# A recommender's GRU phase in program order on all engines, with a reordered phase change and a wider AUGRU tail

## Chip, cores and metric

One core of one Trainium2 chip. The metric is the device time of one execution in microseconds (us), median over the timed runs. Spans, busy times and waits come from the profile of one execution each. The experiments fell on three chips, called A, B and C here; the kernel before takes 2296 to 2299 us on chip A and 2259 to 2261 us on B and C (medians). The chip of the first runs of the two kernels is not recorded; their timed runs agree with chip A's. So kernels of different chips are compared by their ratio to the kernel before in the same rounds, or by stages of their profiles.

Shorthand for engines: PE is TensorE, DVE VectorE, ACT ScalarE, POOL GpSimd, SP SyncE.

## The reference

1024 users, 100 time steps, vectors of 128. A GRU runs over the history; an attention network scores every GRU state against the item; a masked softmax over time gives weights; a second GRU (AUGRU) runs over the GRU's states with these weights; its state at each user's own length goes into a small prediction network.

```python
def gru_step(h, x_t):
    gi = x_t @ gru_Wih.T + gru_bih
    gh = h @ gru_Whh.T + gru_bhh
    ...
    r = sigmoid(i_r + h_r); z = sigmoid(i_z + h_z)
    n = tanh(i_n + r * h_n)
    return (1.0 - z) * n + z * h
keys = scan(gru_step)                                       # 100 steps
feat = concatenate([keys, q, keys - q, q * keys])           # q: the item
score = relu MLP 512 -> 80 -> 40 -> 1 of feat, masked
pooled = einsum('bt,btd->bd', softmax(score over t), keys)
att_seq = pooled.T[:T]
def augru_step(h, (x_t, a_t)):
    r = sigmoid([h, x_t] @ Wr.T + br); u = sigmoid([h, x_t] @ Wu.T + bu)
    h_hat = tanh([h * r, x_t] @ Wh.T + bh)
    u = a_t[:, None] * u
    return (1.0 - u) * h + u * h_hat
hist_sum = (history * mask).sum(1) / length
comb = [user, item, hist_sum, item * hist_sum, AUGRU state at length - 1]
out = sigmoid MLP 640 -> 200 -> 80 -> 1 of comb
```

## The kernel before: the parts concerned

Users lie in the free dimension, in two halves of 512 columns. In the GRU phase a step does the gates of both halves and, one step later, the attention of both (`attend`). The three layers of the attention network for three successive time steps share one PSUM tile, in groups of 32 columns of the weights.

```python
def gru(self, t):                       # one half, one step
    pr = gate(0, both)
    nc.scalar.activation(r, pr, AF.Sigmoid, ...)
    ...
    pz = gate(1, both)
    nc.scalar.activation(pz, pz, AF.Sigmoid, ...)
    u = (ph + bhh) * r                  # VectorE, scalar_tensor_tensor
    nc.vector.tensor_add(pi, pi, u)
    nc.scalar.activation(pi, pi, AF.Tanh, ...)
    nc.vector.tensor_sub(d, h, pi)
    nc.vector.tensor_mul(d, pz, d)
    nc.vector.tensor_add(hn, pi, d)     # the new state
...
def attend(t):                          # 32 matmul records
    ...
    for half in halves:
        nc.vector.tensor_add(f, p[half.i], q0[...])
        nc.scalar.activation(half.mv, f, AF.Relu)
        half.score(t)                   # nc.scalar.dma_start: mv row -> s_b
...
for s in range(T):
    ...
    for half in halves:
        half.load(s + 2); half.load_mask(s + 2)   # x and m, by SyncE
        half.gru(s)
        half.product(s - 1); half.transpose(s - 1)  # kq; keys
        if half.i: attend(s - 1)
        half.stage()                    # softmax, one piece
        ...
        half.history(s)                 # GpSimd: hist += x * m
        half.pool(2, nc.gpsimd)         # GpSimd: pooled += e * key
...
with ExitStack() as pools:
    gru_phase(pools)                    # a scheduler orders the engines
```

The masks come late, so x and m of the first six steps are loaded a second time for `history` (called "again" below). AUGRU sorts users by length and narrows its columns from step to step (`WIDTHS`).

## Time and profile before

| | before |
|---|---|
| timed, median (4 runs) | 2299.15 us (2291.01 to 2299.93) |
| first profile: span, mean granted clock | 2260.6 us, 0.960 |
| last hn of the GRU phase | 1540.8 us |
| last hn to the end of AUGRU step 2 | 87.9 us |
| AUGRU step 2 to the end of the span | 631.9 us |

The lines of this profile are in the prediction. The profile is 1.7% shorter than the timed runs.

### The profile page before, as it was taken

The numbers are of one execution on the slowest core, as the hardware profiler recorded it, in microseconds if no ns is written. First come the engines' busy times: TensorE is split into PE (matmuls) and PEld (weight loads), VectorE is DVE, ScalarE is ACT, GpSimd is POOL, SyncE is SP. The second block draws the span as 40 slices with busy tenths as digits, with TensorE's granted clock in tenths as the row PEclk, the third lists the DMA queues.
The fourth block names the chain that finished last, engine by engine and source line by source line (L and its number), as shares of the span: only waits on it lengthen the run. The fifth ranks groups of instructions, "written<-read, shape, count | busy, mean of one in ns | idle before, by whom it ended". The sixth has DMA issues, their size and how long they took to land. (4 is left out here: it accounts for less than half of the span.)

```text
span 2260.6 us, 26532 instructions
## 1 busy us (share of the span) xinstructions
PE 2124.9 (94%) x8260; PEld 1013.4 (45%) x8260; DVE 1728.9 (76%) x3166; ACT 868.3 (38%) x1545; POOL 1285.2 (57%) x1289
## 2 busy tenths in 40 slices
PE   8898688999999999999999999995899999999998
PEld 3333233333333333333333333332444555679888
DVE  6776667788888888787878787898467877879752
ACT  3233223343433334333333333442343444445542
POOL 0147597676767676767676767694544444443410
PEclk9999899999999999999999999998899999999975
DMA  5344433332332323232323233312533333333310
GB/s 116 64 90 129 127 94 108 99 96 86 95 92 84 105 70 115 74 115 71 109 78 98 77 94 90 92 45 72 149 93 108 97 89 98 101 96 80 82 37 5
DMA packets 253427, 204.64 MB, mean 91 GB/s; under 512 B 74727, under 2 KB 215755, under 8 KB 253275
## 3 DMA queue, kind: packets, MB, share of 16 engines
q1 hardware_dynamic: 239482, 169.03, 27.7%
q0 software_dynamic: 12192, 32.17, 4.9%
q10 hardware_dynamic: 1600, 1.64, 0.2%
q8 instruction: 67, 1.10, 0.2%
q14 instruction: 86, 0.70, 0.1%
HBM read 146.73 MB, written 54.40 MB: 89 GB/s over the span
## 5 line engine op out<-in xcount | busy, mean ns | idle before, releaser
L463 PE MATMUL ps<-x,wih 128*128 128x512 f32 x1200 | 604.1, 613 | 62.2 <-ACT r L475 29.0
L463 PE MATMUL ps<-hn,whh 128*128 128x512 f32 x1188 | 583.2, 600 | 1.3 <-DVE hn L498 1.3
L463 PEld LDWEIGHTS ps<-x,wih 128*128 128x128 f32 x1200 | 220.0, 192 | 396.1 <-issue 214.1
L463 PEld LDWEIGHTS ps<-hn,whh 128*128 128x128 f32 x1188 | 228.4, 193 | 294.0 <-issue 267.6
L704 ACT ACTIVATE mv<-f 128x512 f32<-128x512 f32 (+1 forms) x204 | 128.2, 629 | 495.3 <-DVE f L703 371.7
L450 POOL TENSOR_TENSOR xm<-x,m 128x512 f32<-128x512 f32 x200 | 249.1, 1262 | 102.1 <-PE ps L463 72.6
L494 ACT ACTIVATE ps<-ps,bih 128x512 f32<-128x512 f32 x200 | 132.2, 661 | 400.7 <-DVE ps L493 324.4
L620 POOL TENSOR_TENSOR pooled<-pooled,kw 128x512 f32<-128x512 f32 x190 | 262.9, 1383 | 6.9
L451 POOL TENSOR_TENSOR hist<-hist,xm 128x512 f32<-128x512 f32 x200 | 263.7, 1333 | 2.9
L496 DVE TENSOR_TENSOR d<-hn,ps 128x512 f32<-128x512 f32 x198 | 135.7, 685 | 165.4 <-ACT ps L494 161.5
L605 POOL TENSOR_TENSOR pooled<-pooled,e 128x512 f32<-128x512 f32 x25 | 29.8, 1193 | 366.4 <-ACT e L579 366.4
L679 PE MATMUL pm<-hn,wk 128*32 128x512 f32 x1200 | 230.5, 600 | 6.0 <-DVE f L703 3.4
L152 POOL DMA_INDIRECT rows<-keys_d,idx_k x204 | 196.3, 962 | 69.3 <-issue 35.5
L679 PE MATMUL pm<-kq,wkq 128*32 128x512 f32 x1200 | 227.4, 594 | 0.0
L679 PE MATMUL pm<-mv,w 128*32 128x512 f32 (+1 forms) x808 | 213.5, 606 | 13.4 <-ACT mv L704 10.6
L530 DVE TENSOR_TENSOR kq<-hn,item 128x512 f32<-128x512 f32 x200 | 205.9, 1035 | 4.5 <-PE pm L679 4.3
L619 POOL TENSOR_TENSOR kw<-kt,e 128x512 f32<-128x512 f32 x190 | 207.4, 1110 | 0.5 <-DVE old L586 0.3
L483 DVE SCALAR_TENSOR_TENSOR u<-ps,bhh,r 128x512 f32<-128x512 f32 x198 | 145.8, 737 | 62.9 <-ACT r L475 53.7
L151 POOL COPY rows<-u 128x1 f32<-128x1 f32 x200 | 30.7, 181 | 258.4 <-DVE u L845 257.9
L497 DVE TENSOR_TENSOR d<-ps,d 128x512 f32<-128x512 f32 x200 | 137.9, 689 | 16.0 <-ACT ps L480 0.9
L493 DVE TENSOR_TENSOR ps<-ps,u 128x512 f32<-128x512 f32 x200 | 138.9, 694 | 13.5 <-PE ps L463 0.5
L835 PE MATMUL ph<-r,wh 128*128 128x512 f32 (+55 forms) x396 | 137.1, 430 | 9.5 <-DVE r L841 7.9
(154 smaller groups left out, 3167.0 us busy)
## 6 DMA issues: line engine op xcount, KB each, us to landing
x<-in_hist_x SPq DMA_DIRECT2D x212, 256.0 KB
keys_d<-kt SPq DMA_DIRECT2D x46, 1024.0 KB
m<-mask_d SPq DMA_DIRECT2D x200, 128.0 KB
keys_d<-kt SPq DMA_DIRECT2D x64, 64.0 KB
rows<-keys_d,idx_k POOLq DMA_INDIRECT x204, 2.8
s_b<-mv ACTq DMA_DIRECT2D x200, 8.0 KB
mask_i<-in_mask SPq DMA_DIRECT2D x8, 200.0 KB
at<-att_d SPq DMA_DIRECT2D x4, 256.0 KB
```

The source lines that it names most:

```text
L152: nc.gpsimd.indirect_dma_start(out=r[:, k, :], out_offset=None, in_=keys_d[q], in_offset=bass.IndirectOffsetOnAxis(ap=idx_k[:, k, i : i + ...
L450: nc.gpsimd.tensor_mul(d, x, m)
L451: nc.gpsimd.tensor_add(acc, acc, d)
L463: nc.tensor.matmul(p, lhsT=w[:, g, :], rhs=v, start=(j == 0), stop=(j == len(parts) - 1),)
L483: nc.vector.scalar_tensor_tensor(out=u, in0=ph, scalar=bhh[:, 2:3], in1=r, op0=ALU.add, op1=ALU.mult,)
L493: nc.vector.tensor_add(pi, pi, u)
L497: nc.vector.tensor_mul(d, pz, d)
L530: nc.vector.tensor_mul(kq, h, item[:, self.cols])
L619: eng.tensor_mul(d, k, w)
L620: eng.tensor_add(acc, acc, d)
L679: nc.tensor.matmul(p[i][s, :], lhsT=w[:, s], rhs=v, start=start, stop=stop)
L835: nc.tensor.matmul(p, lhsT=m[:, 0, :], rhs=v, start=False, stop=True)
```

## The change

Its intent: every engine executes the GRU phase in the order of the program text instead of a scheduler's, so attention matmuls are always issued in fours that share the array; preparation comes in small pieces, one per step; the poolings, features and weights at the phase change get a new order; AUGRU never has fewer than 96 columns, spreads its gathers evenly, and gives predictions two PSUM buffers of their own.

```diff
-EIGHTH, FALL = 8, 41
+EIGHTH, FALL, LEAST = 8, 41, 96
-WIDTHS = [[min(HB, 2 * -(-r // (2 * EIGHTH))) for r in room] ...
+    [max(LEAST, min(HB, 2 * -(-r // (2 * EIGHTH)))) for r in room] ...
 ... (preparation in yielded pieces, some of it moved to ScalarE)
-                nc.scalar.activation(pz, pz, AF.Sigmoid, bias=brz[:, 1:2])
 ... (in gru: z now follows tanh, kq stands inside the half)
                 nc.scalar.activation(pi, pi, AF.Tanh, bias=bih[:, 2:3])
+                nc.scalar.activation(pz, pz, AF.Sigmoid, bias=brz[:, 1:2])
+                between()
 ... (in the loop)
-        late = 6
+        late, again = 6, 24
-                half.gru(s)
-                if s:
-                    half.product(s - 1)
+            for half in halves:
+                half.gru(s, lambda: half.product(s - 1) if s else None)
+                if half.i == 0:
+                    for each in halves:
+                        each.stage()
+            for half in halves:
+                half.exponents()
 ...
+                for half in halves:
                     half.transpose(s - 1)
-                if s and half.i:
-                    attend(s - 1)
+                if not staged:
+                    next(rest, None)
+                attend(s - 1)
 ... (after the loop)
-            half.pool(T, nc.vector)
+        for half in reversed(halves):
             half.weights()
         for half in halves:
             half.features()
 ... (AUGRU)
-        ps = ... name="ps3", bufs=8, space=PSUM
+        ps = ... name="ps3", bufs=6, space=PSUM
+        pa = ... name="pa3", bufs=2, space=PSUM    # predictions, weights
-                for _ in range(RATE):
+                for _ in range(due.pop(0) if due else 0):
                     next(ahead, None)
-    with ExitStack() as pools:
+    with ExitStack() as pools, tc.manual_schedule():
         gru_phase(pools)
```

## The prediction

> **What bounds the kernel now.** I read the page's busy slices first, then busy time by stretch, then orders of time (timelines) of single steps, last the waits by engine. The stretches (columns: length, then busy us of PE, PEld, DVE, ACT, POOL, then granted clock, DMA share, GB/s):
>
> ```profile
> 1200.00:1500.00 300.00, 293.06 (x1138) 112.13 (x1140) 250.30 (x388) 119.33 (x184) 210.50 (x171) 0.99 0.32 92
> ...
> 2178.00:2190.00 12.00, 10.72 (x57) 9.86 (x55) 4.96 (x29) 3.91 (x15) 2.23 (x4) 0.64 0.09 24
> 2190.00:2247.00 57.00, 55.98 (x252) 54.09 (x253) 19.46 (x122) 17.48 (x66) 0.00 (x0) 0.50 0.03 6
> ```
>
> In the GRU phase TensorE is busy 98% and VectorE 83%; in the last 57 us of AUGRU the granted clock is 0.50. But 98% is not 98% of the work possible. A timeline of one step shows what the matmuls cost:
>
> ```profile
> 1006.52 1.88 PE L463 MATMUL ps<-x,wih 128*128 128x512 f32 x4
> ...
> 1008.23 1.02 PE L463 MATMUL ps<-hn,whh 128*128 128x512 f32 x2
> ...
> 1014.33 0.62 PE L679 MATMUL pm<-hn,wk 128*32 128x512 f32 x2
> ...
> 1014.35 0.62 PE L679 MATMUL pm<-mv,w 128*32 128x512 f32 x2
> ...
> 1014.79 0.60 PE L679 MATMUL pm<-hn,wk 128*32 128x512 f32 x2
> ```
>
> Four gate records take 1008.23 - 1006.52 = 1.71 us, 0.43 us each; well packed, four attention records of 32 columns start together every 0.43 to 0.46 us. A GRU step has 24 gate records (12 matmuls, two records each) and 32 attention records (the groups of costliest instructions: 3208 in 100 steps), so 24 + 32/4 = 32 slots of 0.43 = 13.7 us. The writes of hn give what a step takes: step 30 ends at 522.7, step 99 at 1540.8, 14.75 us each. So 1.0 us per step is lost to attention matmuls that come one by one. The first 31 steps took 522.7, some 65 us more than 31 times 14.75: preparation and DMA waits. From the last hn to the first full AUGRU step (PE at 1602.5) pass 61.7 us; AUGRU takes the remaining 658.
>
> **What the Trainium skill says.** "TensorE: Matmul & The Clock Gate", "Architectural detail": only PE may pull weight loads ahead; ScalarE and VectorE are strict FIFO. Here the order of two short queues decides everything. The same page, Part 1: little activity drops the clock to half; the trace agrees, 0.50 from 2190. "ScalarE: Activation LUTs", "What ACT_TABLE_LOAD costs": about 1283 ns plus a drain; the trace has 1.28. "SBUF — State Buffer", "Who interferes with whom": VectorE with two SBUF inputs blocks against GpSimd reads; the trace agrees: kq (two SBUF inputs) has median 0.82 but mean 1.035 and longest 1.74, while d, f and hn, each with an input in PSUM, stay at 0.65 to 0.69.
>
> **The change, part by part.**
>
> *GRU in program order.* The built order of the changed kernel is, per step, on VectorE: u, add, kq, d, d, hn for half 0, then a softmax stage if one is due, the same six for half 1, two transposes, two adds f. On ScalarE: r, tanh, sigmoid z for half 0, for half 1, exponentials if due, relu 0, its s_b DMA, relu 1, its DMA, then the next r. That closes a loop: the next u stands behind both f and needs r, and r stands behind both relus and DMAs, which need f. Its length comes from these lines:
>
> ```profile
> 251.93 0.71 DVE L483 SCALAR_TENSOR_TENSOR u<-ps,bhh,r 128x512 f32<-128x512 f32 x1
> 252.74 0.70 DVE L493 TENSOR_TENSOR ps<-ps,u 128x512 f32<-128x512 f32 x1
> 254.17 0.69 DVE L496 TENSOR_TENSOR d<-hn,ps 128x512 f32<-128x512 f32 x1 [0.73 <-ACT ps L494]
> 254.96 0.69 DVE L497 TENSOR_TENSOR d<-ps,d 128x512 f32<-128x512 f32 x1
> 255.69 0.69 DVE L498 TENSOR_TENSOR hn<-ps,d 128x512 f32<-128x512 f32 x1
> ```
> ```profile
> 1007.33 1.28 DVE L703 TENSOR_TENSOR f<-pm,q 128x512 f32<-128x512 f32 x2
> ...
> 1008.04 0.63 ACT L704 ACTIVATE mv<-f 128x512 f32<-128x512 f32 x1 [3.51 <-DVE f L703]
> 1008.69 1.28 ACT L475 ACT_TABLE_LOAD   x1
> ```
> ```profile
> 1026.39 0.50 ACTq L540 DMA_DIRECT2D s_b<-mv  x1
> 1026.94 0.63 ACT L704 ACTIVATE mv<-f 128x512 f32<-128x512 f32 x1 [5.83 <-DMA m<-mask_d]
> ```
>
> One half: u to add 0.81, add to d 1.43 (tanh in between, which kq fills), then 0.79, 0.73 and 0.61 until something independent may start: 4.37. Two halves 8.74, two transposes 2 x 0.635, two f 1.28: 11.29 of VectorE. After the start of the pair, f 0 ends at 0.68, relu 0 runs 0.71 to 1.34, its DMA holds the queue 0.50 (second fence of ScalarE: the next instruction starts 0.55 after the DMA), relu 1 1.92 to 2.55, DMA to 3.08, r 3.13 to 3.82, u at 3.86: 2.58 after the pair's end. A step without softmax is 11.29 + 2.58 = 13.87 us, already level with TensorE's 13.7. Softmax adds to it, because the stage stands in VectorE's row: scores 0.72 + 0.27 + 0.27 + 0.17 + 0.16 + 0.28 = 1.87, sums 0.33 + 0.25 + 1.01 + 0.93 = 2.52 (mean durations of the groups from 500 to 1500), both for two halves in 8 steps: +1.10. The table reload ahead of r: 1.28 x 2/8 = +0.32. kq under contention: I take +0.2. Sum: 15.5 us per step, **longer than the 14.75 of now**. TensorE's loss of packing goes away, but it will wait instead.
>
> Sum of the phase: hn of step 0 at 17 (16.7 now), 99 x 15.5 = 1534, less 14 for some ten early steps without softmax, plus 19 for preparation left on VectorE (8 rank counts 10.1, on 1.9, order 1.8, used 1.2, alive 1.0, small ones 3), plus 8 for the early steps in which s_b's DMA waits behind key writes: last hn at 1564, **+23** against 1540.8. The first 31 steps gain some 40 of it, the other 69 lose 52 and more. The pieces do remove the two 12 to 13 us stalls of now (idx_k waiting 12.4 for place_i, a d waiting 12.9).
>
> *Phase change.* Two queues for 8 pooled_d writes (6.6 us of issue on one now) and fewer separate softmax ends; but the features, now spread into the GRU's end, come after, with four GpSimd products of 1.28 ahead of the gathers. **-5.**
>
> *AUGRU on 96 columns.* Order of time of the h writes, half by half:
>
> ```profile
> 2160.97 0.26 DVE L851 TENSOR_TENSOR h<-h,ph 128x108 f32<-128x108 f32 x1
> ...
> 2164.27 0.26 DVE L851 TENSOR_TENSOR h<-h,ph 128x102 f32<-128x102 f32 x1
> ...
> 2185.96 0.22 DVE L851 TENSOR_TENSOR h<-h,ph 128x72 f32<-128x72 f32 x1
> ...
> 2191.92 0.22 DVE L851 TENSOR_TENSOR h<-h,ph 128x66 f32<-128x66 f32 x1
> ```
>
> At 102 columns a step takes 3.30 us, at 66 to 72 it takes 5.96, because the clock has halved. Steps 83 to 99 take 82.4 us now; 17 at 3.45, the rate of 98 columns, are 58.7: **-24**, if 96 keep the clock.
>
> *Gathers and PSUM.* Steps 8, 15, 22 and 30, at ends of blocks of keys, take 1.5 to 2.4 us over the trend; the even spread ends the gathers a step earlier: **-7**. Steps 27, 52 and 77, with the final predictions, are 5.5 to 7.3 us over it; with buffers of their own the predictions interleave with gates in the built order: **-9**. Six buffers instead of eight suffice for gates (three per half step).
>
> Sum: +23 - 5 - 24 - 7 - 9 = -22, so 2260.6 becomes 2239, -1.0%. The timed runs are 1.7% above the profiled one; with the same ratio 2299.66 x 0.990 = 2277. I say **2280**.
>
> **Rivals.**
> 1. TensorE sets the pace. Program order packs attention perfectly, and a step is 13.9: 99 x 13.9 + 17 + 19 = 1412, so -129 with -45 after: 2087, timed about 2125. For it: 98% busy and the purpose of the change. Against: TensorE is not in the loop worked out above; only durations that shrink could free it. In part (15.0 per step) it gives 2228 timed.
> 2. DMA waits move into ScalarE. Its s_b DMAs wait for earlier DMAs of the same semaphore; now they stop ScalarE, in order, for 76 us between 500 and 1500 (mv waiting, laid to m loads). If they stay, +0.7 per step: 2347. Against: GpSimd, whose lag delays the m loads now, has 10.5 us of work in a longer step, and loads are issued at the start of a step.
> 3. 96 columns do not hold the clock: the 24 are lost, 2304.
>
> **Range and chances.** The loop holds for given durations, so I do not see the GRU phase get much shorter; at 15.2 without contention all is 2245, at 16 some 2328. Unknown waits widen this: **2215 to 2330**. Faster by over 2% (below 2254) 0.25, within 2% 0.66, slower 0.09.
>
> **What would show it.** Right: hn writes 15 to 16 us apart in the middle, TensorE down to 88 to 90% there, idle mostly ahead of hn and kq matmuls; VectorE idle ahead of u by about 2.5 us each step, laid to r; first 31 steps faster, the rest slower; clock 1.00 at 2190 and after, steps of 3.4 to 3.5 at the end. Wrong: steps of 14 us or less with TensorE still at 98%, or ScalarE waiting for DMA by over 1 us per step.

## More of the kernel before

The stages are read off the timeline: a GRU step ends with its second write of hn, an AUGRU step with its second write of h.

The profiled execution took 2262.48 us and is none of the four timed ones; that is the time of chips B and C, and its stages fit theirs as well (see e5 and e15). So it may come from another chip than the timed runs; the record does not say.

## The result, and the profile after

The changed kernel takes 2373.7 us (2370.04 to 2380.84, 4 runs) against 2299.15. The ratio is 1.0336, with a 95% interval of 1.0303 to 1.037: slower by 3.4%. Ratios are the mean time of one kernel's fast runs over that of the other's of the same rounds, so not quite the ratio of the medians. The predicted 2280 and its range up to 2330 were too low. On chip C the changed kernel later took 2350.35 us, 1.0408 of the kernel before.

The profiled span is 2368.3 us. By stages, with a second profile of the kernel before from chip A beside the first:

| us | before, 1st profile | before, 2nd profile (chip A) | after |
|---|---|---|---|
| steps 1 to 24, mean | 17.37 | 17.23 | 15.81 |
| steps 25 to 48, mean | 14.61 | 14.61 | **17.36** |
| steps 49 to 95, mean | 14.83 | 14.81 | **15.74** |
| last hn | 1540.8 | 1537.2 | **1619.0** |
| last hn to AUGRU step 2 | 87.9 | 96.8 | **137.2** |
| AUGRU steps 3 to 83 | 539.4 | 563.4 | 543.0 |
| AUGRU steps 84 to 99 | 78.8 | 78.4 | 56.2 |
| span | 2260.6 | 2289.4 | 2368.3 |

Against the second profile, whose time is that of the timed runs, the change loses 82 us in the GRU phase and 40 at the phase change and gains 43 in AUGRU, some 79 in all. The medians of the timed runs differ by 75.

**The GRU phase.** The stretch of which the prediction shows the row of before, 1200 to 1500 us (columns as there):

```profile
1200.00:1500.00 300.00, 284.48 (x1096) 107.16 (x1094) 227.81 (x359) 110.57 (x168) 192.99 (x157) 0.98 0.29 85
```

TensorE is busy 284.5 of 300 us instead of 293.1, but with 1096 records instead of 1138: its busy time per record is no shorter (0.260 against 0.258 us). So the matmuls are not packed better here, and TensorE waits more.

The row of u in the groups of costliest instructions, before and after (behind the first bar busy time and mean duration, behind the second the idle time of VectorE ahead of it, with the releaser of most of it):

```profile
L483 DVE SCALAR_TENSOR_TENSOR u<-ps,bhh,r 128x512 f32<-128x512 f32 x198 | 145.8, 737 | 62.9 <-ACT r L475 53.7
```
```profile
L499 DVE SCALAR_TENSOR_TENSOR u<-ps,bhh,r 128x512 f32<-128x512 f32 x198 | 147.9, 747 | 328.9 <-ACT r L492 312.9
```

VectorE stood 62.9 us ahead of u in the whole phase, now 328.9, 3.3 us per step, and nearly all of it waits for r. An ordinary step shows the loop. Timeline of VectorE, then of ScalarE, around 1084 us (start, duration; in brackets the idle time before and what ended it):

```profile
1083.76 1.25 DVE L731 TENSOR_TENSOR f<-pm,q 128x512 f32<-128x512 f32 x2
1087.63 0.75 DVE L499 SCALAR_TENSOR_TENSOR u<-ps,bhh,r 128x512 f32<-128x512 f32 x1 [2.62 <-ACT r L492]
```
```profile
1084.44 0.63 ACT L732 ACTIVATE mv<-f 128x512 f32<-128x512 f32 x1 [3.48 <-DVE f L731]
1085.10 0.50 ACTq L558 DMA_DIRECT2D s_b<-mv  x1
...
1086.36 0.50 ACTq L558 DMA_DIRECT2D s_b<-mv  x1
1086.91 0.69 ACT L492 ACTIVATE r<-ps,brz 128x512 f32<-128x512 f32 x1 [0.58 <-PE ps L480]
```

The two f end at 1085.01; between them and r stand relu 0, its DMA, relu 1 and its DMA; u starts at 1087.63, 2.62 us after the f.

Steps 24 to 48 are another matter. Step 43, counted from 0, took 23.2 us (699.7 to 722.9). Its lines on SyncE's queue, ScalarE and VectorE:

```profile
684.20 0.42 SPq L455 DMA_DIRECT2D m<-mask_d  x1
705.88 0.33 SPq L450 DMA_DIRECT2D x<-in_hist_x  x1
```
```profile
701.56 0.63 ACT L732 ACTIVATE mv<-f 128x512 f32<-128x512 f32 x1 [4.23 <-DVE f L731]
708.95 0.50 ACTq L558 DMA_DIRECT2D s_b<-mv  x1
709.55 0.63 ACT L732 ACTIVATE mv<-f 128x512 f32<-128x512 f32 x1 [7.36 <-DMA m<-mask_d]
```
```profile
712.05 0.75 DVE L499 SCALAR_TENSOR_TENSOR u<-ps,bhh,r 128x512 f32<-128x512 f32 x1 [9.93 <-ACT r L492]
```

SyncE issues nothing for 21 us; relu 0 is done at 702.2, but its DMA goes out only at 708.95, after loads that SyncE issued at 705.88 and later; r and u follow. In these steps SyncE's queue waited 130.0 us for GpSimd's history products, which free the buffers of x and m (the waits of that queue, 395 to 812 us; 2.3 us from 812 to 1230). It waited longer for transposed keys, 160.8 us, but that is no less in the ordinary stretch (262.6). The sum alone says little: the kernel before has 239.7 us of waits for history products in the same window, but none over 8.7 us, where the longest here is 18.9.

What ties the two queues stands in the trace's own records of waits. A DMA raises a counter, its completion semaphore, when it lands. The DMAs of SyncE and ScalarE share eight of them, and 168 of the 200 s_b DMAs have a wait for their own semaphore right before them. The one of 708.95 waits for semaphore 104, on which the x load of 705.88 lands at 708.87; the one of 710.78 waits for semaphore 110, on which the x load of 706.78 lands at 710.71. So an s_b DMA is held until the load before it on its semaphore has landed.

**The phase change.** SyncE's queue and GpSimd, before and after:

```profile
1577.31 6.58 SPq L635 DMA_DIRECT2D pooled_d<-att  x8
```
```profile
1586.21 0.99 POOL L128 DMA_INDIRECT att_r<-pooled_d,idx  x1 [28.03 <-DMA pooled_d<-att]
```
```profile
1669.67 2.53 SPq L661 DMA_DIRECT2D pooled_d<-s_b  x4
1672.31 0.89 SPq L667 DMA_DIRECT2D rlen<-rlen_d  x1
...
1686.64 0.45 SPq L667 DMA_DIRECT2D rlen<-rlen_d  x1
...
1699.74 0.37 SPq L690 DMA_DIRECT2D part_d<-part  x1
```
```profile
1700.11 0.99 POOL L132 DMA_INDIRECT att_r<-pooled_d,idx  x1 [6.63 <-PE pk L868]
```

From the first pooled_d write to the first gather of weights pass 30.4 us instead of 8.9. The features of the two halves lie between, one after the other: the second rlen load stands in SyncE's order behind the part_d write of the first half. The pooled_d writes themselves begin 50.7 us after the last hn instead of 36.5. GpSimd has 19 pooling instructions left there instead of 13, and it waits for the softmax twice, 11.30 and 11.35 us; which of the two makes the 14 us is not shown. On chip C the same two pieces make up the whole difference: e13 (the changed kernel) against e14 (phase change of before) has 50.6 against 36.6, 29.2 against 8.9, and 118.8 against 84.7 in all.

**AUGRU.** The last steps keep their clock (columns as above):

```profile
2296.00:2355.00 59.00, 48.57 (x399) 45.62 (x397) 42.61 (x196) 29.07 (x102) 10.39 (x18) 1.00 0.26 41
```

### The profile page after: what moved, and what is told of

Read it like the earlier page. It is cut to its first block, busy times and chain, and to the rows that moved or that the text cites. A ratio compares the mean times of both kernels' runs of the same rounds, so it can differ in the third digit from the quotient of the medians.

```text
span 2368.3 us, 26550 instructions
## 1 busy us (share of the span) xinstructions
PE 2128.7 (90%) x8260; PEld 988.5 (42%) x8260; DVE 1727.8 (73%) x3155; ACT 873.3 (37%) x1547; POOL 1289.7 (54%) x1297
## 5 line engine op out<-in xcount | busy, mean ns | idle before, releaser
L480 PE MATMUL ps<-x,wih 128*128 128x512 f32 x1200 | 615.3, 623 | 28.6 <-ACT r L492 24.3
L499 DVE SCALAR_TENSOR_TENSOR u<-ps,bhh,r 128x512 f32<-128x512 f32 x198 | 147.9, 747 | 328.9 <-ACT r L492 312.9
L480 PEld LDWEIGHTS ps<-hn,whh 128*128 128x128 f32 x1188 | 233.2, 196 | 298.9 <-issue 295.1
L705 PE MATMUL pm<-kq,wkq 128*32 128x512 f32 x1200 | 221.8, 635 | 91.7 <-DVE kq L548 91.6
L732 ACT ACTIVATE mv<-f 128x512 f32<-128x512 f32 x200 | 125.9, 630 | 440.5 <-DVE f L731 349.1
L705 PE MATMUL pm<-mv,w 128*32 128x512 f32 (+1 forms) x808 | 219.2, 606 | 17.1 <-DVE e L587 14.8
L548 DVE TENSOR_TENSOR kq<-hn,item 128x512 f32<-128x512 f32 x200 | 194.8, 975 | 0.0
L492 ACT ACTIVATE r<-ps,brz 128x512 f32<-128x512 f32 x200 | 137.6, 688 | 56.7 <-PE ps L480 38.1
L884 PE MATMUL ph<-r,wh 128*128 128x96 f32 (+47 forms) x396 | 131.4, 414 | 19.6 <-DVE r L890 19.2
```

The source lines that it names most:

```text
L480: nc.tensor.matmul(p, lhsT=w[:, g, :], rhs=v, start=(j == 0), stop=(j == len(parts) - 1),)
L492: nc.scalar.activation(r, pr, AF.Sigmoid, bias=brz[:, 0:1])
L499: nc.vector.scalar_tensor_tensor(out=u, in0=ph, scalar=bhh[:, 2:3], in1=r, op0=ALU.add, op1=ALU.mult,)
L548: nc.vector.tensor_mul(kq, h, item[:, self.cols])
L705: nc.tensor.matmul(p[i][s, :], lhsT=w[:, s], rhs=v, start=start, stop=stop)
```

## The experiments

Unless said otherwise: correct, ratio to the kernel before of the same rounds.

### e1 to e4, chip A: is it the order, and is it the loop?

**e1_scheduled.**

```diff
-    with ExitStack() as pools, tc.manual_schedule():
+    with ExitStack() as pools:
         gru_phase(pools)
```

> The changed kernel with the scheduler let loose again on the GRU phase (only the program-order mode is taken away; pieces, order of code, phase change and AUGRU stay). Loop theory (the fixed order closes f, relu, DMA, relu, DMA, r, u into a loop): the GRU phase falls back to about 14.8 us per step, last hn at 1500 to 1550 instead of 1619, and the phase change gets back some 30 of its 49 us because the scheduler pulls features into the GRU's end; about 2250 to 2300 us. Rival (the rewritten code itself costs, e.g. z after tanh, kq inside the half, 'again' loads at 24): last hn stays above 1600 and the time near 2370.

Measured: 2210.88 us, ratio 0.961 (0.9573 to 0.9647). Last hn at 1487.7, means 14.75 (25 to 48) and 14.34 (49 to 95), phase change 104.4. The program-order mode alone costs the changed kernel 163 us, more than expected: the rewritten code, freely scheduled, is better than the kernel before. The rival (the rewritten code costs) is out.

**e2_before_gru_after_augru.** GRU phase and phase change of the kernel before, AUGRU of the changed one.

> GRU phase and phase change of the kernel before, AUGRU of the changed one (96 columns, even spread, PSUM buffers of its own for predictions). If the AUGRU part is worth what the changed kernel's trace shows from step 2 on (about 20 us), 2275 to 2282 us; if it is worth what the prediction gave it (40), about 2260. If its gain depends on the rest of the change (a GRU that ends late lets something finish), no change, 2299.

Measured: 2255.74 us, ratio 0.9803 (0.9767 to 0.984), so 43 us: about the 40 of the prediction, though its own profile (span 2262.1) is no shorter than the first profile of before. That contradiction led to e5.

**e3_before_program_order.** The kernel before with the program-order mode added, nothing else.

> The kernel before with program order alone for its GRU phase: nothing rewritten. Loop theory: program order is the cost and the rewriting a repair of part of it, so this is slower than the changed kernel: in each half product and transposes stand in VectorE's row ahead of the next half's u, z stands ahead of tanh in ScalarE's, and the preparation is in big lumps: 16 to 17.5 us per step, last hn 1650 to 1800, 2400 to 2550 us. If the rewriting costs and program order does not: faster than the changed kernel, about 2300.

Measured: 2800.54 us, ratio 1.2173, 20.18 us per step. The direction is right, the size far outside: the mode costs the unchanged code 502 us and the rewritten one 163, so the rewriting takes away most of the cost of program order. Which part of it does so was not taken apart.

**e4_f_and_relu_one_step_later.** Both f, both relus and their DMAs go into half 0 of the next step.

```diff
+                def between():
+                    if s:
+                        half.product(s - 1)
+                    if pend and half.i == 0:
+                        pend[0]()               # both f, behind kq
+                half.gru(s, between)
                 if half.i == 0:
                     for each in halves:
                         each.stage()
+                    if pend:
+                        pend[1]()               # relus and s_b DMAs, behind z
...
-                attend(s - 1)
+                pend = attend(s - 1, True)
```

> The changed kernel with both f, both relus and their s_b DMAs moved from the end of a step into half 0 of the next step (f behind kq, relus behind z), still program order. This opens the loop: the next r no longer stands behind relus that wait for f. Loop theory: outside the 'again' steps 24 to 48 a step falls from 15.8 to 14.2 to 14.6 us (VectorE's own 12.7, a bubble of 0.5 ahead of u of half 1, TensorE 13.7), last hn about 1480 to 1530, whole 2230 to 2290 us; VectorE's idle ahead of u falls from 3.3 us per step to under 1.5. DMA-wait theory (s_b DMAs waiting for loads stop ScalarE everywhere): the step stays near 15.8 since the same DMAs stand in the same queue ahead of r of half 1. In both, the spikes of 20 to 25 us in steps 24 to 48 stay.

Measured: 2226.47 us, ratio 0.9686 (0.965 to 0.9722), 147 us less than the changed kernel and a little better than expected. Last hn at 1463.6; means 14.42, 15.66 and 14.11 in the three stretches. The row of u:

```profile
L499 DVE SCALAR_TENSOR_TENSOR u<-ps,bhh,r 128x512 f32<-128x512 f32 x198 | 148.3, 749 | 190.6 <-PE ps L480 126.2
```

The wait is shorter, 1.9 us per step (under 1.5 was expected), and most of it is now for TensorE's matmuls, not for r: TensorE is the bound, busy 300.0 of 300 us from 1100 to 1400. The same DMAs stand in the same queue, so the DMA-wait theory does not explain the ordinary steps; but four of the five spikes of over 20 us in steps 24 to 48 are still there, with 19 to 25 us (27, 31, 35 and 43; step 47 has 14.5). A slip in this version, found later: the score of step 98 goes into a buffer whose block (92 to 95) has not been read yet. The comparison of results did not notice it; e9 repairs it.

### e5 to e8, chip A: the other terms

**e5_before_again.** The kernel before, unchanged.

> The kernel before, unchanged, profiled once more. Its first profile had a span of 2260.6 us at a mean clock of 0.960, but its timed runs took 2291 to 2309 at 0.950 to 0.956, while the changed kernel's profile and timed runs agree within 0.5%. If the difference lies in the narrow last steps of AUGRU (clock halved from an earlier step on), this profile is near 2298 us and the extra 38 us stand between step 60 and step 99, GRU unchanged (last hn at 1541). If it lies in the GRU phase, the last hn comes later than 1550.

Measured: 2299.68 us (2 runs), span of the profile 2289.4. The GRU phase is as before. The extra time is in AUGRU, but earlier than expected: steps 3 to 83 take 24.0 us more (563.4 against 539.4), steps 84 to 99 none (78.4). The phase change takes 9 more. Two stretches of it:

```profile
2140.00:2148.00 8.00, 5.58 (x40) 4.92 (x39) 5.06 (x20) 2.27 (x7) 6.58 (x13) 1.00 0.45 118
2148.00:2156.00 8.00, 5.80 (x27) 5.25 (x26) 3.69 (x14) 2.66 (x8) 1.86 (x2) 0.60 0.28 67
```

TensorE is busy only 5.58 of 8 us, and in the next 8 us its clock is 0.60: an idle stretch, and then, from 2149.6 for 6.8 us, half clock. The Trainium skill, "TensorE: Matmul & The Clock Gate", "HAM oscillation — how this bites in real kernels", has it that a wait that outlasts the activity window (some 3.4 us) makes the next work start cold. The trace agrees in part only: no single wait is that long here. The three before 2149.6 are 1.35, 0.80 and 0.82 us, and the one before the next half clock, at 2187.1, is 2.49. The clock is not all of the 24 us either: over steps 3 to 83 TensorE is idle 29.1 us instead of 13.4, and its busy time, with 23.9 us at half clock instead of 3.4, grows from 526.0 to 534.3. What makes it idle there is not shown.

The first profile has no such places between steps 53 and 83. All three profiles of kernels with common PSUM buffers on chip A have them (e3, e5, e6: 568.6, 563.4 and 565.8 for steps 3 to 83); the first profile, with 539.4, is nearer to those of chips B and C (e12, e15: 544.0 and 545.2, with the even spread). Its phase change, 87.9, is theirs too (86.8 and 87.6; 96.8 to 99.3 in e2, e5 and e6 on A).

**e6_before_with_96.** The kernel before with `max(LEAST, ...)` in `WIDTHS` alone.

> The kernel before with at least 96 columns alone (no even spread, no PSUM buffers of their own for predictions). If 96 columns are all of the gain of the AUGRU part (steps 2 to 83 of the changed kernel, 543.0 us, were no shorter than before, 539.4) and its other parts cost some 12 us at the start of AUGRU, this is at 2240 to 2252 us, faster than before's GRU with the whole new AUGRU part (2255.7). If the spread and the buffers are worth the 16 us that the prediction gave them, 2265 to 2275.

Measured: 2270.54 us, ratio 0.9878 (0.9859 to 0.9897): 26 us. Steps 84 to 99 fall from 78.4 to 58.2; steps 3 to 83 stay at 565.8, with the clock drops. The time lies in the second range, 2265 to 2275: 96 columns bring some 20 to 26 us, and spread and buffers together another 15 on this chip. They are not only the waits that the prediction meant: from e6 to e2 TensorE's idle time in steps 3 to 83 falls from 29.2 to 19.1 us, and its busy time, with fewer clock drops, from 536.6 to 524.2.

**e7_history_reload_own_buffer.** The second loads of x and m get a buffer pair of their own, one every four steps.

```diff
+        ag = pools.enter_context(tc.tile_pool(name="ag", bufs=1))
-                    x = xp.tile([P, HB], F32, name="x")
+                    x = (ag if again else xp).tile([P, HB], F32, name="x")
 ... (the same for m)
-            n, odd = divmod(s - again, 2)
+            n, odd = divmod(s - again, 4)
-            if 0 <= n < late and odd:
+            if 0 <= n < late and odd == 2:
                 halves[i].history(n)
```

> The changed kernel with the second loads of x and m of the first six steps in a buffer of their own and one every four steps (24 to 71) instead of every two (24 to 47); nothing else. DMA-wait theory for this stretch (the loads take buffers of the common rotation, so x loads of the coming step wait for GpSimd's history products of the step before; SyncE stands, and the s_b DMAs on ScalarE with it): the mean step of 24 to 48 falls from 17.36 to 15.8 to 16.0 us, spikes over 19 us go, last hn 1619 to some 1580 to 1585, whole 2330 to 2342 us. Rival (GpSimd's own load, not the buffers): the stretch keeps its mean of 17 or passes it to 48 to 72; no gain over 10 us.

Measured: 2345.59 us, ratio 1.0211 (1.0186 to 1.0236): 28 us less than the changed kernel. Steps 25 to 48 fall from 17.36 to 16.04 and steps 49 to 95 stay (15.73); last hn at 1587.6. No step of the stretch is over 19 us any more, and the slow stretch is not passed on to later steps. So the buffers and rate of the second loads cause it. The run changes both together and does not say which matters more.

**e8_features_ahead.** rlen and user loads right behind the loop; feature products on VectorE and matmuls ahead of the last poolings.

```diff
+        for half in halves:
+            half.ready()          # rlen and user loads
         for half in halves:
             half.product(T - 1)
...
         attend(T + 1)
+        for half in halves:
+            half.features()
...
             half.weights()
-        for half in halves:
-            half.features()
```

> The changed kernel with the features moved: rlen and user loads right behind the loop, the four products on VectorE and the matmuls behind the last attend, ahead of the last poolings, instead of behind the pooled_d writes. If the features in series after the weights are what delays the first gather (1700.1, 30.5 us after the first pooled_d write; 9 us before the change), the gather starts some 10 us after that write, the phase change falls from 137 to 112 to 118 us, whole 2348 to 2356 us. If the wait has another cause (all DMAs of the phase, SyncE's order), under 8 us are gained.

Measured: 2349.66 us, ratio 1.0228 (1.0205 to 1.0251), 24 us less; phase change 113.4 instead of 137.2. SyncE's queue and GpSimd:

```profile
1656.05 5.77 SPq L695 DMA_DIRECT2D part_d<-part  x2
1672.97 2.52 SPq L661 DMA_DIRECT2D pooled_d<-s_b  x4
```
```profile
1679.26 0.99 POOL L132 DMA_INDIRECT att_r<-pooled_d,idx  x1 [10.84 <-DMA pooled_d<-s_b]
```

The part_d writes are over before the pooled_d writes, and the gather follows after 6.3 us instead of 30.4, waiting for pooled_d itself. The features in series were the cause.

### e9 to e12, chip B

**e9_loop_open_reload_phase.** e4 and e7 together, with the phase change rewritten: loads and products of the features first, features ahead of the last poolings, block ends `92, 96, T` instead of `92, 96, 98, T`.

> Program order kept, with everything found so far: f and relu in half 0 of the next step, history reload in its own buffer every four steps, and the phase change rewritten (rlen and user loads and the four feature products first, features ahead of the last poolings, the last three softmax blocks made two, so 96 to 99 are one block; this also repairs a slip of the run with f and relu one step later, where the score of step 98 could overwrite that of step 92 before it was read). From the terms measured: step 0 at 16, 99 steps of 14.1 to 14.2 us give a last hn of 1412 to 1425 (1463.6 without the reload's buffer); first pooled_d write 38 to 46 us later, AUGRU step 2 at about 95 to 105 us after hn, AUGRU 605 to 612: 2115 to 2145 us. If the gains do not add (TensorE at its 13.7 us meets another limit, or GpSimd's reload still holds up loads), last hn stays at 1440 or later.

Measured: 2141.12 us, ratio **0.947** (0.9455 to 0.9486). Last hn at 1431.9, means 14.42, 14.42 and 14.12; phase change 99.1. The GRU phase in the middle:

```profile
1100.00:1400.00 300.00, 299.64 (x1202) 114.31 (x1200) 253.72 (x403) 124.97 (x187) 208.91 (x169) 1.00 0.34 98
```

TensorE is busy 299.6 of 300 us, with 1202 records instead of the 1096 of the changed kernel in as many us. The terms add up, except that last hn is 7 us later than expected.

**e10_the_same_scheduled.** e9 without the program-order mode.

> The kernel of the run before (loop opened, reload, phase change) with the scheduler in place of program order. If program order is worth something once its loop is open (tight packing of the attention matmuls), this is slower: steps of 14.4 to 14.8 us as the scheduled runs had, last hn 1450 to 1490, 2160 to 2210 us. If the order of code was all and the scheduler only repairs or keeps it, both are within 10 us.

Measured: 2216.1 us, ratio 0.9811 (0.979 to 0.9833); 14.73 us per step from 49 to 95, last hn at 1515.3. That is just over the expected range. With the loop open, program order gains 75 us.

**e11_s_b_from_sync.** In the changed kernel, `nc.scalar.dma_start(out=s_b...` becomes `nc.sync.dma_start(out=s_b...`.

> The changed kernel with the s_b DMAs issued from SyncE instead of ScalarE, nothing else. Loop theory with the sizes of the prediction: behind the pair of f the path is relu 0, relu 1, r, u without the two DMA issues of 0.5 us, so the bubble ahead of u falls from 2.58 to about 1.45 us, and a step from 15.8 to 14.6 to 14.8 us outside 24 to 48; last hn 1619 to 1510 to 1530; whole 2260 to 2290. If ScalarE's DMA issues are not in the loop (r waits for its matmuls anyway), under 0.3 us per step, last hn above 1590. Risk in both: SyncE now waits for relu and issues x loads later, which can lengthen the spikes of 24 to 48.

Measured: 2214.72 us, ratio 0.9805 (0.9775 to 0.9835). Means 14.82, 15.23 and 14.57; last hn at 1487.3 (1510 to 1530 expected). An ordinary step on VectorE:

```profile
1205.70 1.25 DVE L731 TENSOR_TENSOR f<-pm,q 128x512 f32<-128x512 f32 x2
1208.22 0.75 DVE L499 SCALAR_TENSOR_TENSOR u<-ps,bhh,r 128x512 f32<-128x512 f32 x1 [1.27 <-ACT r L492]
```

The gap between the f and u is 1.27 us instead of 2.62, near the 1.45 expected, and the step in the ordinary stretch is 1.17 shorter. The risk did not come true, on the contrary: steps 25 to 48 lose 2.1 us each. With e7 this shows both ends of the second mechanism: the loads are late because of the buffers, and ScalarE is stopped by them because its own DMAs wait for their semaphores. The phase change is 17 us shorter too; that was not followed up.

**e12_before_96_spread_common_psum.** e2 with eight common PSUM buffers.

> GRU of the kernel before, AUGRU with 96 columns and the even spread, but eight common PSUM buffers as before (no buffers of their own for predictions). 96 columns alone gave 2270.5, all three parts 2255.7. If the spread brings the 15 us (no full gather queue beside AUGRU's steps), 2254 to 2258; if the buffers of their own bring it (predictions at steps 52 and 77 interleaved with gates, so TensorE does not idle and lose its clock), 2268 to 2273; in between if both.

Measured: 2244.49 us, ratio 0.9932 (0.9915 to 0.9948), on another chip than e2 and e6, where the kernel before is 38 us faster. The question could not be answered across chips, hence the next four.

### e13 to e16, chip C

**e13_after_same_chip.** The changed kernel, unchanged.

> The changed kernel again, because the runs so far fell on two chips on which the kernel before took 2298 and 2261 us: is the difference the chip's, and does the changed kernel have it too? If the chip only touches the narrow AUGRU steps of the kernel before (idle stretches of TensorE, then half clock), this is 2365 to 2375 us on either chip; so 1.033 of before on the one and 1.048 on the other. If the chip as a whole is slower, the changed kernel keeps its ratio, and takes 2335 us on the fast one.

Measured: 2350.35 us, ratio 1.0408 (1.0391 to 1.0425). Between the two expectations: the chip is worth 23 us here, 38 for the kernel before. Last hn is the same (1617.7); the phase change is 18 us shorter (118.8), most of it between the last gather of weights and the end of AUGRU step 0 (8.1 us instead of 22.7), AUGRU 3 to 83 by 6 (536.7).

**e14_before_96_own_psum.** e2 with `return [2] * (NH * T)` in place of the even spread: two gathers per half step as before.

> GRU of the kernel before, AUGRU with 96 columns and PSUM buffers of their own for predictions, but two gathers per half step as before (no even spread). On the chip where before takes 2298: 96 columns alone 2270.5, all three 2255.7. If the buffers of their own keep TensorE's clock, near 2256; if not, near 2270. Where before takes 2261, no idle stretches are to be saved, and this is at 2240 to 2246 like the run with the spread (2244.5).

Measured: 2218.27 us, ratio 0.9819 (0.9802 to 0.9835), better than both expectations.

**e15_before_96_spread_again.** The kernel of e12.

> The even spread with common PSUM buffers once more, on the same chip as the run with the buffers of their own, for comparison: if the spread saves the idle stretches, 2254 to 2258 where before takes 2298; where before takes 2261, 2244 as measured.

Measured: 2245.0 us, ratio 0.9938 (0.9921 to 0.9954), like e12. So the buffers of their own bring the gain and not the spread: e14 takes 531.5 us for steps 3 to 83 where e15 takes 545.2, and 53.0 for steps 84 to 99 at a clock of 1.00 where e15 takes 63.3 at 0.87. Ends of step 51 and step 52 (predictions) in e14, then in e15 (the write of h of the second half):

```profile
2015.48 0.43 DVE L853 TENSOR_TENSOR h<-h,ph 128x262 f32<-128x262 f32 x1
...
2024.09 0.41 DVE L853 TENSOR_TENSOR h<-h,ph 128x256 f32<-128x256 f32 x1
```
```profile
2020.70 0.43 DVE L852 TENSOR_TENSOR h<-h,ph 128x262 f32<-128x262 f32 x1
...
2031.63 0.41 DVE L852 TENSOR_TENSOR h<-h,ph 128x256 f32<-128x256 f32 x1
```

8.6 us with buffers of their own, 10.9 with common ones. Steps 27, 52 and 77 together take 34.8 in e15 (35.7 in the first profile of before) and 25.1 in e14. The even spread moves waits rather than saving them: it shortens steps 8, 22 and 30 (12.3, 10.9 and 9.6 us to 9.7, 8.2 and 7.6) and lengthens steps 55, 63 and 70 (4.9, 4.5 and 3.8 to 7.3, 7.8 and 5.7, e14 against e16). The runs e14 and e15 differ in both parts; e16 has both of them, behind another GRU phase. Over steps 3 to 83 e15 takes 545.2, e16 535.0 and e14 531.5: with the spread, the buffers save 10.2, and with the buffers, the spread costs 3.5.

**e16_loop_open_same_chip.** The kernel of e9 beside the changed one.

> The fastest kernel so far (loop opened, reload in its own buffer, phase change rewritten, program order) on the same chip as the changed one: 2141 us as before if the chip touches only the kernel before, since its AUGRU is that of the changed kernel; then 0.902 of the changed kernel's time. If the whole chip is slower than the other, 2170 to 2180.

Measured: 2139.42 us, ratio 0.9474 (0.9458 to 0.9491). By the medians on this chip that is 0.910 of the changed kernel. It beats the kernel before on two chips, and the changed kernel on this one.

## Why the prediction was wrong

The loop that it named is there, near the size that it worked out. Two steps failed: it argued rival 2, DMA waits in ScalarE, away, and it gave the phase change -5 without adding up the features. The prediction's sum was +23 (GRU phase) - 5 (phase change) - 40 (AUGRU) = -22 us; measured against the second profile it is +82 + 40 - 43 = +79.

- **The loop (right).** "11.29 + 2.58 = 13.87, ... 15.5 us per step": measured 15.74 in steps 49 to 95. The 2.58 of the gap measured 2.62. e4 opened the loop (14.11), e11 shortened it by the two DMA issues, by the worked-out amount. Program order was meant to help TensorE; in this text it tied TensorE to a chain of VectorE and ScalarE that is longer than TensorE's own work.
- **First steps faster, rest slower (right in sign).** The first 31 steps end at 493.2 instead of 522.7, a gain of 29.5. The prediction's "some 40" does not come out of its own terms, which give 17 + 30 x 15.5 - 14 + 19 + 8 = 495, a gain of 28. The other 69 steps lose 108 instead of 52.
- **Rival 2, DMA waits in ScalarE (rejected, and right for 24 steps).** This is the step that failed in the GRU phase. The prediction argued against it: "GpSimd ... has 10.5 us of work in a longer step, and loads are issued at the start of a step". It overlooked that the change moves the second loads to steps 24 to 47, where they take buffers of the common rotation while GpSimd pools as well. Its own sign of being wrong, ScalarE waiting for DMA by over 1 us per step, came true there: 38.4 us from 395 to 812 us, 1.6 per step (3.1 in all from 1000 to 1400). Cost: 24 x (17.36 - 15.74) = 39 us. Together with 0.24 x 75 = 18 for the ordinary steps this is about the difference between 1564 and 1619 (55; the first steps gain 2). e7 takes 31 of it away, and e11 shows how it reaches VectorE.
- **Phase change, "-5" (wrong).** It is +40 on chip A (137.2 against 96.8). The prediction said that the features "come after" and did not add up what that means: SyncE's order puts the second half's loads behind the first half's write. e8 gives 24 back. Another 14 stand ahead of the first pooled_d write, 50.7 against 36.5 us; their cause is open, and e9 does not remove them (54.1 us to that write): its 99.1 in all comes from the 6.0 us from there to the first gather, and e16 (99.0) shows the same on the chip on which the changed kernel takes 118.8.
- **96 columns, "-24" (right in size).** Steps 84 to 99: 78.8 to 56.2, the clock 1.00. e6 alone confirms it (58.2). But 96 columns do not always hold the clock, so rival 3 is true in part: in other kernels with them these steps take 53.0 (e14) to 64.3 (e2), with a clock of 1.00 and 0.87. Nor does the row of 2190 to 2247 show "little activity": TensorE is recorded busy 55.98 of 57 us at the clock of 0.50.
- **Gathers "-7" (wrong), PSUM "-9" (right in size on the fast chips).** The spread brings nothing (535.0 against 531.5), the buffers 7.9 (539.4 to 531.5, first profile against e14). On chip A they also go with fewer idle stretches and clock drops: 565.8 (e6) to 543.3 (e2), but e2 has the spread too, so which of the two does it there is open. That AUGRU gains 43 in all, near the predicted 40, is luck: against the first profile, from which the 40 was worked out, it gains 19 (618.2 to 599.2); the rest are the idle stretches and clock drops of the second one, which the prediction did not know.
- **Profile to timed runs by a factor (wrong).** The prediction multiplied 2299.66 by 0.990, as if the excess of 1.7% were the same for both kernels. The first profile of before has no clock drops in steps 53 to 83; the second, with the usual time, has them, and the changed kernel's profile (2368.3) is only 0.2% below its timed runs.
- **TensorE "down to 88 to 90%" (wrong).** It is busy 95% from 1200 to 1500 us. The row of 1200 to 1500 shows why that is no comfort: fewer records, each busy as long (0.260 against 0.258 us). "TensorE's loss of packing goes away" was wrong too; it went away only with the loop open (e9: 1202 records in 299.6 us). Attention matmuls and their weight loads waited for kq 63.4 us between 1000 and 1400 us in the changed kernel and 10.5 in e4 (waits by engine).
- **Rival 1 (TensorE sets the pace, 13.9)** did not happen, but the number was good: e9 reaches 14.12.

## What to carry to other kernels

Before fixing an order, write each in-order engine's queue for one iteration and follow the chains that cross engines twice: work of the last iteration that stands in a queue ahead of the next iteration's first instruction closes a loop, and moving it to a place where its engine waits anyway opens it. A DMA in a compute engine's queue is a wait for whatever that DMA waits for, here for the landing of the last DMA on the same completion semaphore, which can be one of another queue. When a change moves preparatory work to another stretch, ask whose buffers it borrows there, and when it puts a branch of work "after", add up that branch's own chain.

## What the Trainium skill lacked or had wrong

- "TensorE: Matmul & The Clock Gate" describes the idle stretch and the half clock that follows for waits longer than the activity window; in e5 half clock follows several waits of 0.8 to 1.35 us within 5 us, and one of 2.49. The page has nothing on its dependence on the chip. The same kernel took 2298.93 and 2296.4 us on chip A and 2260.7 and 2258.98 on B and C; on chip A steps 3 to 83 of AUGRU took 24 us more than in the first profile (563.4 against 539.4), some 16 of them TensorE's idle time and 8 its longer busy time.
- I found on no page that DMAs of SyncE and ScalarE can share completion semaphores, so that one issued from ScalarE waits for a load issued from SyncE to land and stops the activations behind it: 7.36 us in one step of the changed kernel. It would belong to "DMA: Bandwidth & Descriptors". With those DMAs on SyncE, steps 25 to 48 took 2.1 us less each, of which 1.17 is what ordinary steps gained too (e11). Here the program's own waits make the tie (semaphores 104 and 110 in step 43), not the DMA hardware.
